# A planned attention kernel: final maxima queued at once, additions until the last pair, and another order of heads in the scores

## The chip, the cores and the metric

The kernel runs on one core of one Trainium2 chip. The metric is the time of one execution in microseconds on the device. Before the change it is 5001.09 us, the median of 3 runs (5000.94 to 5010.77). The core has five engines that run side by side, each with its own queue of instructions: TensorE (matrix products; "PE" in the profile, and "PEld" for its weight loads), VectorE (DVE), ScalarE (ACT), GpSimd (POOL) and SyncE (SP, which issues the transfers).

## The reference

The input x has 8 batches of 1024 rows of 512 numbers, and a context of 8 x 1024 x 384. Cut to what matters:

```
# layer 1: cross-attention to the context, 8 heads of 64
y = layernorm(x); q = y @ Wq; k = ctx @ Wk; v = ctx @ Wv
x = x + tanh(g1) * (softmax(q k^T / 8) v @ Wo + bo)

# layer 2: self-attention, 16 heads of 32, and a gate per row
y = layernorm(x); q, k, v = y @ Wq.T + bq, y @ Wk.T + bk, y @ Wv.T + bv
q = (q / |q| + query_embedding) * softplus(temperature)
h = softmax(q k^T / sqrt(32)) v
gates = softmax(h @ Wr.T + br), the 3 largest of 15 kept; sw = softmax(h @ Ws.T + bs)
weight = sum of 3 * gates * 2 sw[1], and 2 sw[0] * sum(sw)
x = x + tanh(g2) * ((h * weight) @ Wp.T + bp)
```

All of it is float32.

## The kernel before, in words

**Tiling.** A batch has 8 tiles of 128 rows. Features stand on the partitions in attention. A *chunk* (class `Chunk`, line 261) is 128 of the 512 head features: two heads of 64 in layer 1 (kind 1), four heads of 32 in layer 2 (kind 2). Each layer of each batch has four chunks, so there are 64 chunks, worked off one after the other. Queries are taken in two halves of 512.

**A chunk's steps.** `attention` (582) goes through the steps of a chunk: 8 in kind 1, 16 in kind 2. A step covers one half of the queries and two key tiles (kind 1) or one (kind 2). `score` (441) makes four score products of 128 keys x 512 queries, in two PSUM tiles of two each (`sc`, two buffers). The negative maximum of each query row is added by a product with one row of ones (`ones_b`, line 454), and then comes k times q. Each head has its own strip of 32 or 64 rows of the array. ScalarE takes the exponential of each of the two tiles (465). `value` (541) multiplies the exponentials with v (552), one step behind the scores: the scores of step m+1 are issued before the values of step m.

**The sums.** Softmax needs the sum of the exponentials over keys. GpSimd adds two exponential tiles (`paired`, 468 and 470: two key tiles in kind 1, the tiles of two steps in kind 2). Then `add` (474) either lets VectorE add the result to a running one (483), which frees a buffer, or keeps it as one more item. `summed` (493) reduces all kept items over the partitions with products with ones (503): a round of two or four products for every kept item. Its result's reciprocal comes from ScalarE (527, 528), and `divided` (531) multiplies the chunk's output with it, mostly on GpSimd. The exponential tiles have nine buffers; `room` (631) forces a reduction (`summed` with a partial result, 516 and 524) if too many are kept.

**The maxima.** While a chunk is attended to, the row maxima of the next one are found in bf16 (`maxima`, 371): pairs of score products (`pm`, 378; two heads each) and VectorE's maximum of each (419), or four at once in the wide form (402). In kind 2, pairs with n = 0 are of heads 0 and 1 and those with n = 1 of heads 2 and 3. At the end VectorE takes the negative maximum over all key halves (`nm`, 424), TensorE transposes it (`pr`, 428), ScalarE copies it (430), and four DMAs by SyncE (432) write it to rows of `sh`, which the scores of that chunk read.

**Order by a planner.** The order on TensorE, ScalarE, VectorE and GpSimd is the order in which the program issues the instructions. The program keeps a planned time for TensorE, VectorE and GpSimd in `at`, and each piece of work adds its planned cost. `attend` (674) interleaves the steps of a chunk with maxima pairs of the next chunk or the one after it (`pair`, 659) and with *fillers* (projections, output products, transposes of other stages). A pair is issued only if VectorE's planned time is not more than a given slack ahead of TensorE's; for the last two calls (`nm` and `pr`) the slack is 0. Work that others must finish first is put on lists with a due time (`later`, `soon`). `in_time` (701) tells by the number of pairs still to come whether VectorE may do additions in kind 2 and in batch 0; in kind 1 of later batches it may at all times. `pace` (978) does the same between the layers, and in the prologue, with fillers alone.

**The rest that is touched.** `gates` (828) makes the gate products (`pg`) of one half of the queries once the last chunk of that half is in `finished`. The prologue (1002 to 1026) normalises the eight tiles of batch 0, transposes them (`pt`, 218), and puts one tile of the context's v (`pv`) between two of these; then come the projections of the first chunks.

Of the kernel before, what the change touches and what calls it, by code (L numbers as in the profile page):

```python
# [10 lines left out]
F32 = mybir.dt.float32  # L11
# [5 lines left out]
P = 128  # L17
# [4 lines left out]
def tile_gated_block(  # L22
# [41 lines left out]
    NT = N // P  # L64
    ND = D // P
    NDC = DC // P
    H = 512
    NH = N // H
    NQ = NT // NH
# [155 lines left out]

    part = [False]

    columns = [HD2]
# [32 lines left out]
    class Chunk:  # L261
# [109 lines left out]
        def maxima(self):  # L371
# [35 lines left out]
            while todo:  # L407
                c, kh, n = todo.pop(0)
                if wide[0] and (kh if nh == 2 else n) == 0:
                    todo.pop(0)  # L410
                    four(c, kh)
                    self.done += 1
                    yield
                    continue
                at["PE"] = max(at["PE"], at["DVE"] - 700)
                for i in (2 * n, 2 * n + 1):
                    ps = gen(f"pm_{key}_{i}_{c}_{kh}")
                    scores(ps, c, i, kh)
                    nc.vector.tensor_reduce(mx[:, i * NT + c, kh : kh + 1], ps, AX.X, ALU.max)  # L419
                pe(PAIR)  # L420
                dve(2 * 690)
                yield
            nm = small.tile([P, nh * NT], F32, tag="nm", name=f"nm_{key}")
            nc.vector.tensor_reduce(nm, mx, AX.X, ALU.max, negate=True)
            dve(200)
            yield
            pr = ps_gen.tile([nh * NT, P], F32, tag="gen", name=f"pr_{key}")
            nc.tensor.transpose(pr, nm, ident)
# [11 lines left out]

        def score(self, step):

            h, s = step
            kind, nh, width, key = self.kind, self.nh, self.width, self.key
            pss = [
                ps_sc.tile([P, 2, H], F32, tag="sc", name=f"sc_{key}_{h}_{s}_{u}") for u in range(2)
            ]
            parts = [(i, kk) for kk in range(self.nk) for i in range(nh)]
            for m in range(2):
                for j, (i, kk) in enumerate(parts):  # L450
                    r, kc = i * width, s * self.nk + kk
                    if m == 0:
                        r += kk * HD2
                        lhsT, rhs = ones_b[r : r + 1, :], self.sh[r : r + 1, ts(h, H)]
                    else:
                        rows = slice(r, r + width)
                        lhsT, rhs = self.k[rows, ts(kc, P)], self.q[rows, ts(h, H)]
                    nc.tensor.matmul(  # L458
                        pss[j // 2][:, j % 2, :], lhsT=lhsT, rhs=rhs, start=(m == 0), stop=(m == 1)
                    )  # L460
            pe(self.SC)
            e = []
            for u in range(2):
                e.append(epool.tile([P, 2, H], F32, tag="e", name=f"e_{key}_{h}_{s}_{u}"))
                nc.scalar.activation(e[u], pss[u], AF.Exp)  # L465
            self.e[step] = e

# [63 lines left out]
        def divided(self, h, r=None):  # L531

            if h not in self.halves:
                self.halves[h] = r
                return
            self.finished.add(h)
            hT, r = self.st.hT[h][:, self.c, :], self.halves[h] if r is None else r
            engine = nc.vector if self.ends else nc.gpsimd
            engine.tensor_tensor(hT, hT, r, ALU.mult)
# [61 lines left out]

        def begun(self):
            self.whole = {}
            self.e, self.acc, self.parts, self.halves, self.finished = {}, {}, {}, {}, set()
            self.score(self.steps[0])


# [51 lines left out]
    def pair(ch, slack):  # L659

        if ch is None or ch.mx is None or at["PE"] < ch.free:
            return False
        if ch.done + 2 >= ch.pairs:
            slack = 0
        elif part[0]:
            slack = min(slack, 700)
        if at["DVE"] - at["PE"] > slack:
            return False
        ch.done += 1
        if next(ch.mx, "end") == "end":  # L670
            ch.mx = None
        return True

    def attend(
# [146 lines left out]
    def finish(st, other=None):  # L821
# [180 lines left out]
    st = begin(0)  # L1002
# [102 lines left out]
```

## Time and profile before

| | |
|---|---|
| median of 3 runs | 5001.09 us |
| profiled execution, its own time | 5004.68 us |
| its span, first to last instruction | 5002.9 us |
| mean granted clock of TensorE | 0.996 |
| TensorE busy | 4803.4 us (96%) |
| VectorE, GpSimd, ScalarE busy | 2988.2, 2567.5, 2309.3 us |
| additions of exponentials on VectorE (line 483) | x431, 760.1 us |
| sums on TensorE (line 503) | x1364 records, 204.2 us |

A row of the groups gives line, engine, operation, output and inputs, shapes and count, then busy time and the mean of one in ns, then idle time of the engine before these and what ended it. A row of the waits gives who waited for whom: us in total, times, and the longest. A row of the timeline gives the start and the duration in us, and in brackets the idle time before it. A row of the table by stretch gives its ends and length, the busy time of TensorE, its weight loads, VectorE, ScalarE and GpSimd with counts, the granted clock, the DMA share and GB/s. A float32 product leaves two records, a bf16 one leaves one.

### The profile page before, as it was taken

The page shows a single profiled execution, that of the slowest core. Times are in us where ns is not written, and L with a number is a line of the kernel's source. Part 1 is how long each engine was busy: PE and PEld are TensorE (multiplying, and loading weights), DVE is VectorE, ACT ScalarE, POOL GpSimd, SP SyncE. Part 2 cuts the span into 40 slices and gives each one's busy share as a digit, 9 for nine tenths or more (in the row PEclk, how much of TensorE's full clock was granted, in tenths as well). Part 3 has the DMA queues.
Part 4 walks back from the last instruction along what each step waited for, and adds up shares of the span by engine and source line. Part 5 has one row for each costly group of instructions (what it writes and reads, how often), then busy time and mean ns, then how long its engine had stood idle before and what let it go on. Part 6 is the DMA issues. An engine that isn't in the chain of part 4 may idle for free.

```text
span 5002.9 us, 83870 instructions
## 1 busy us (share of the span) xinstructions
PE 4803.4 (96%) x35660; PEld 1427.7 (29%) x35660; DVE 2988.2 (60%) x4111; ACT 2309.3 (46%) x3036; POOL 2567.5 (51%) x1346
## 2 busy tenths in 40 slices
PE   9999999999999999999999999999999999999998
PEld 2222232222322223222233222332223322233222
DVE  4657755577555775557745577555765557654664
ACT  3435634356343563435634356243652436524354
POOL 1635646356463663636636366363663636636464
PEclk9999999999999999999999999999999999999999
DMA  2000010000101001010010100101001010010000
GB/s 79 26 29 19 24 50 27 33 17 23 49 26 36 14 23 49 26 36 13 23 55 20 36 13 23 64 11 36 17 21 64 9 36 22 9 51 9 18 1 18
DMA packets 126280, 145.18 MB, mean 29 GB/s; under 512 B 14544, under 2 KB 75984, under 8 KB 125904
## 3 DMA queue, kind: packets, MB, share of 16 engines
q1 hardware_dynamic: 125616, 139.81, 8.8%
q8 instruction: 279, 4.57, 0.4%
q14 instruction: 97, 0.79, 0.1%
q10 hardware_dynamic: 288, 0.00, 0.0%
HBM read 122.47 MB, written 16.78 MB: 28 GB/s over the span
## 4 chain that ended last, share of the span: by engine, by line
PE 78%; DVE 9%; ACT 7%; issue 4%; POOL 2%; DMA 1%; SPq 0%; ACTq 0%; DVEq 0%; POOLq 0%
PE sc L458 21%; PE av L552 16%; PE po L247 8%; PE pq L247 8%; PE pm L378 7%; PE pk L247 6%; PE pv L247 6%; ACT e L465 5%; DVE mx L402 4%; PE sum L503 3%; DVE mx L419 3%; POOL e L470 2%; PE pt L218 1%; DVE e L483 1%; PE pn L247 1%
## 5 line engine op out<-in xcount | busy, mean ns | idle before, releaser
L470 POOL TENSOR_TENSOR e<-e,e 128x1024 f32<-128x1024 f32 x764 | 1859.3, 2448 | 1230.9 <-PE av L552 767.5
L465 ACT ACTIVATE e<-sc 128x1024 f32<-128x1024 f32 x1536 | 1490.3, 1021 | 1359.6 <-PE sc L458 1290.8
L419 DVE TENSOR_REDUCE mx<-pm 128x1 f32<-128x512 f32 x2336 | 1496.3, 685 | 981.6 <-PE pm L378 969.2
L458 PE MATMUL sc<-q,k 32*128 32x512 f32 (+1 forms) x6144 | 1113.2, 606 | 0.0
L552 PE MATMUL av<-e,v 128*32 128x512 f32 (+1 forms) x6144 | 1080.9, 611 | 0.0
L483 DVE TENSOR_TENSOR e<-e,e 128x1024 f32<-128x1024 f32 x431 | 760.1, 1779 | 347.2 <-POOL e L470 345.4
L378 PE MATMUL pm<-kb,qb 32*128 32x512 bf16 (+1 forms) x3072 | 625.5, 383 | 60.4 <-DVE mx L402 25.9
L402 DVE TENSOR_REDUCE mx<-pm 128x2 f32<-128x1024 f32 x368 | 425.3, 1218 | 290.5 <-PE pm L378 290.5
L458 PE MATMUL sc<-sh,ones_b 1*128 1x512 bf16 x3072 | 406.6, 384 | 76.0 <-ACT e L465 63.7
L458 PEld LDWEIGHTS sc<-q,k 32*128 32x128 f32 (+1 forms) x6144 | 422.6, 186 | 192.4 <-issue 186.2
L378 PEld LDWEIGHTS <-qb 32*128 32x128 bf16 (+1 forms) x3072 | 147.5, 92 | 941.7 <-issue 932.5
L552 PEld LDWEIGHTS av<-e,v 128*32 128x32 f32 (+1 forms) x6144 | 194.0, 117 | 621.2 <-issue 590.4
L247 PE MATMUL pq<-y1T,wq 128*32 128x512 f32 (+1 forms) x1568 | 248.0, 599 | 4.4 <-ACT k L333 2.5
L247 PE MATMUL pk<-y2T,wk 128*32 128x512 f32 x2048 | 242.6, 595 | 7.5 <-ACT qq L320 7.5
L247 PE MATMUL pq<-y2T,wq 128*32 128x512 f32 x2048 | 245.0, 596 | 2.8 <-ACT rn L345 2.8
L247 PE MATMUL pv<-wv,y2T 128*32 128x512 f32 x2048 | 241.3, 597 | 0.0
L247 PE MATMUL po<-wo,h1T 128*32 128x512 f32 x2048 | 229.7, 595 | 1.0
L247 PE MATMUL po<-wp,h2T 128*64 128x512 f32 (+1 forms) x1152 | 230.6, 597 | 0.0
L458 PEld LDWEIGHTS <-ones_b 1*128 1x128 bf16 x3072 | 100.3, 91 | 445.7 <-issue 427.9
L247 PE MATMUL pk<-ctx,wk 128*32 128x512 f32 (+1 forms) x1176 | 190.7, 607 | 17.9 <-DMA ctx<-in_ctx 6.6
L503 PE MATMUL sum<-e,ones 128*32 128x512 f32 (+1 forms) x1364 | 204.2, 596 | 0.0
L347 POOL TENSOR_TENSOR qq<-qq,rn 128x512 f32<-128x512 f32 x64 | 88.3, 1379 | 220.0 <-ACT rn L346 220.0
(109 smaller groups left out, 2871.0 us busy)
## 6 DMA issues: line engine op xcount, KB each, us to landing
x<-in_x SPq DMA_DIRECT2D x64, 256.0 KB
out<-x SPq DMA_DIRECT2D x64, 256.0 KB
xs<-in_x SPq DMA_DIRECT2D x56, 256.0 KB
xn<-in_x SPq DMA_DIRECT2D x56, 256.0 KB
ctx<-in_ctx SPq DMA_DIRECT2D x7, 1536.0 KB
wq<-in_L_xattn_Wq SPq DMA_DIRECT2D x32, 256.0 KB
wo<-in_L_xattn_Wo SPq DMA_DIRECT2D x8, 1024.0 KB
wk<-in_L_ffn_Wk SPq DMA_DIRECT2D x32, 256.0 KB
```

The costliest lines, as they stand in the source:

```text
L218: nc.tensor.transpose(pt[:, c, :], xn[:, ts(c, P)], ident)
L247: nc.tensor.matmul(ps[ts(j, w), :], lhsT=lhsT[:, ts(j, w)], rhs=rhs, start=start, stop=stop)
L347: nc.gpsimd.tensor_tensor(self.qq, self.qq, rn, ALU.mult)
L378: nc.tensor.matmul(ps, lhsT=self.qb[ts(i, width), ts(c, P)], rhs=self.kb[ts(i, width), ts(kh, H)], start=True, stop=True,)
L402: nc.vector.tensor_reduce(out, tiles[u], AX.X, ALU.max)
L419: nc.vector.tensor_reduce(mx[:, i * NT + c, kh : kh + 1], ps, AX.X, ALU.max)
L458: nc.tensor.matmul(pss[j // 2][:, j % 2, :], lhsT=lhsT, rhs=rhs, start=(m == 0), stop=(m == 1))
L465: nc.scalar.activation(e[u], pss[u], AF.Exp)
L470: nc.gpsimd.tensor_tensor(one, one, two, ALU.add)
L483: nc.vector.tensor_tensor(accs[-1], accs[-1], a, ALU.add)
L503: nc.tensor.matmul(ps[ts(2 * u + j, self.width), :], lhsT=ones[:, 0 : self.width], rhs=acc[n][:, j, :], start=(n == 0), stop=(n == len(acc ...
L552: nc.tensor.matmul(self.av[ts(i, width), :], lhsT=st.v[:, kc, ts(self.c * self.nh + i, width)], rhs=e[j // 2][:, j % 2, :], start=(kc == 0 ...
```

## The change

There are six edits.

1. `pair`: the two last calls of a chunk's maxima are no longer held back by VectorE's planned time. `nm` is issued at the next chance, and sets `free` to VectorE's planned end plus 300 ns; the transpose `pr` is issued once TensorE's planned time has reached that.
2. `in_time`: additions are allowed when fewer than two calls are left (only `pr`, or nothing); the bound on pairs is three per step rather than two while a chunk of kind 1 is attended to; the reserve is 7000 ns rather than 10000.
3. `score`: if the last maxima pair issued before it had n = 0 and the chunk is of kind 2, the two PSUM tiles, their products and their exponentials are taken in the order heads 2, 3 and then 0, 1. `value` and the additions keep their order.
4. `divided` notes the planned time at which a half was finished, and `gates` waits until 2500 ns of planned TensorE time after it (not once the last chunk is through).
5. Prologue: the first query projection half stands ahead of the sixth tile's place among the transposes, and there is no v tile in the eighth; the two v tiles left over come later.
6. `pace` in the prologue counts six more products as left.

```diff
@@ maxima @@
+                taken[0] = n == 0
                 pe(PAIR)
                 dve(2 * 690)
                 yield
             nm = small.tile([P, nh * NT], F32, tag="nm", name=f"nm_{key}")
             nc.vector.tensor_reduce(nm, mx, AX.X, ALU.max, negate=True)
             dve(200)
+            self.free = at["DVE"] + 300
             yield
@@ score @@
-            pss = [
-                ps_sc.tile([P, 2, H], F32, tag="sc", name=f"sc_{key}_{h}_{s}_{u}") for u in range(2)
-            ]
-            parts = [(i, kk) for kk in range(self.nk) for i in range(nh)]
+            order = (1, 0) if taken[0] and self.kind == 2 else (0, 1)
+            taken[0] = False
+            pss = {
+                u: ps_sc.tile([P, 2, H], F32, tag="sc", name=f"sc_{key}_{h}_{s}_{u}") for u in order
+            }
             for m in range(2):
-                for j, (i, kk) in enumerate(parts):
+                for j in (2 * u + v for u in order for v in range(2)):
+                    kk, i = divmod(j, nh)
                     r, kc = i * width, s * self.nk + kk
...
-            for u in range(2):
-                e.append(epool.tile([P, 2, H], F32, tag="e", name=f"e_{key}_{h}_{s}_{u}"))
+            e = {}
+            for u in order:
+                e[u] = epool.tile([P, 2, H], F32, tag="e", name=f"e_{key}_{h}_{s}_{u}")
                 nc.scalar.activation(e[u], pss[u], AF.Exp)
@@ divided @@
-            self.finished.add(h)
+            self.finished[h] = at["PE"]
@@ pair @@
-        if ch.done + 2 >= ch.pairs:
-            slack = 0
-        elif part[0]:
-            slack = min(slack, 700)
-        if at["DVE"] - at["PE"] > slack:
-            return False
+        if ch.done + 2 < ch.pairs:
+            if at["DVE"] - at["PE"] > (min(slack, 700) if part[0] else slack):
+                return False
@@ in_time @@
-            steps = (1 - share) * len(ch.steps)
-            return pairs <= 2 * steps - 3 and work <= (1 - share) * (1.1 * total + cost) - 10000
+            steps = (1 - share) * len(ch.steps) * (2 if ch.kind == 2 else 3)
+            return pairs < 2 or pairs <= steps - 3 and work <= (1 - share) * (1.1 * total + cost) - 7000
@@ gates @@
-            while h not in st.chunks[2][-1].finished:
+            done = st.chunks[2][-1].finished
+            while h not in done or not st.through and at["PE"] < done[h] + 2500:
                 yield
@@ prologue @@
-        run(values, NDC * MM)
+        if t == NQ + 1:
+            run(fill, ND * MM)
+        elif t < NT - 1:
+            run(values, NDC * MM)
...
-    pace(one[0], fill, one[1], (14 + 14) * MM)
+    pace(one[0], fill, one[1], (6 + 14 + 14) * MM)
```

More of the change, by code (lines that the diff above doesn't have):

```diff
@@ L226, in tile_gated_block @@
     part = [False]
+    taken = [False]
     columns = [HD2]
@@ L443, in score @@
             h, s = step
-            kind, nh, width, key = self.kind, self.nh, self.width, self.key
-            pss = [
-                ps_sc.tile([P, 2, H], F32, tag="sc", name=f"sc_{key}_{h}_{s}_{u}") for u in range(2)
-            ]
-            parts = [(i, kk) for kk in range(self.nk) for i in range(nh)]
+            nh, width, key = self.nh, self.width, self.key
+            order = (1, 0) if taken[0] and self.kind == 2 else (0, 1)
[3 more added lines that the diff above has]
+            }
             for m in range(2):
-                for j, (i, kk) in enumerate(parts):
+                for j in (2 * u + v for u in order for v in range(2)):
+                    kk, i = divmod(j, nh)
                     r, kc = i * width, s * self.nk + kk
@@ L461, in score @@
             pe(self.SC)
-            e = []
-            for u in range(2):
-                e.append(epool.tile([P, 2, H], F32, tag="e", name=f"e_{key}_{h}_{s}_{u}"))
+            e = {}
+            for u in order:
+                e[u] = epool.tile([P, 2, H], F32, tag="e", name=f"e_{key}_{h}_{s}_{u}")
                 nc.scalar.activation(e[u], pss[u], AF.Exp)
@@ L603, in begun @@
             self.whole = {}
-            self.e, self.acc, self.parts, self.halves, self.finished = {}, {}, {}, {}, set()
+            self.e, self.acc, self.parts, self.halves, self.finished = {}, {}, {}, {}, {}
             self.score(self.steps[0])
```

## The prediction

> **What bounds the kernel now.** I read the page first (busy time and clock by slice), then TensorE's waits, then the timeline at places that the change touches. The page:
>
> ```profile
> span 5002.9 us, 83870 instructions
> PE 4803.4 (96%) x35660; PEld 1427.7 (29%) x35660; DVE 2988.2 (60%) x4111; ACT 2309.3 (46%) x3036; POOL 2567.5 (51%) x1346
> ...
> PE 78%; DVE 9%; ACT 7%; issue 4%; POOL 2%; DMA 1%; SPq 0%; ACTq 0%; DVEq 0%; POOLq 0%
> ...
> L503 PE MATMUL sum<-e,ones 128*32 128x512 f32 (+1 forms) x1364 | 204.2, 596 | 0.0
> ```
>
> TensorE is busy 96% and holds most of the chain; all its idle time is 5002.9 - 4803.4 = 200 us. Time falls only by less work on TensorE or fewer of its waits. VectorE has 40% to spare. The last row is the work that the change takes away: sums of exponentials over keys, as products with ones. The waits of TensorE that the change touches:
>
> ```profile
> PE sc L458 <- ACT e L465: 63.7, 155, 2.1
> PE pm L378 <- DVE mx L419: 21.6, 36, 2.6
> PE sc L458 <- DMA sh<-rows: 10.6, 20, 2.5
> PE pg L247 <- DVE h2T L539: 2.9, 1, 2.9
> ```
>
> None is large: at most 10.6 and 2.9 us can be won at the last two.
>
> **Part 1: additions allowed to the last pair (in_time).** In the built order the sums on TensorE fall from 682 to 590 products, and VectorE's additions rise from 431 to 477. By the tiles: in each batch 0 to 6 the sum of the last second-layer chunk's second half was two groups of 8 products (four rounds of four, in four column strips) and becomes one group of 4 (one round): 3 rounds x 7 = 21. The first chunk of all goes from four rounds to one: 3. In all 24. What a round costs:
>
> ```profile
> 2507.49 1.07 PE L552 MATMUL av<-e,v 128*32 128x512 f32 x8
> 2508.37 1.90 PE L503 MATMUL sum<-e,ones 128*32 128x512 f32 x16
> 2510.09 1.04 PE L247 MATMUL pq<-y1T,wq 128*32 128x512 f32 x8
> ```
>
> From 2508.37 to 2510.09 two rounds took 1.72, so 0.86 each (x16, as each f32 product leaves two records). 24 x 0.86 = 20.6; seven groups fewer, which alone take 0.97 rather than 0.86, 0.8 more: -21.4. Seven partial sums also lose their copy (ScalarE) and their 0.69-us addition (VectorE), off the path.
>
> What of this is given back? Behind this sum come three steps with only scores and values (2.2 us of TensorE), in which scores wait 0.52 us for exponentials. The step that loses the sum has 3.0 us left against 3.17 of the score-exponential-score round trip (2514.42 to 2517.58 between second-half scores), so it gives back about 0.15, and the next chunk's first step, from which a maxima pair moves away, about 0.2: 7 x 0.35 = +2.5. The new order of maxima pairs and projections among steps is worth a little less switching, about -0.5 in all. Part 1: -19.4.
>
> VectorE pays 46 x 1.78 us (row L483: 760.1/431) = 82 us. Does that hold up TensorE? Six additions per batch stand behind the last maximum of the next chunk, ahead of the maxima after it:
>
> ```profile
> 2505.43 0.19 DVE L424 TENSOR_REDUCE nm<-mx 128x16 f32<-128x32 f32 x1
> 2521.24 1.29 DVE L419 TENSOR_REDUCE mx<-pm 128x1 f32<-128x512 f32 x2 [15.63 <-PE pm L378]
> ```
>
> VectorE stood idle for 15.63 us just there. Six additions at this stretch's mean of 2.41 us (slowed beside GpSimd) take 14.4. The last two need GpSimd's pair at 2516.83 to 2521.49, which moves 1.8 earlier with the values before it: done by about 2522. The sum now stands after six projection products of the next chunk's second step, by my count at 2525.7. Cover 3 us; if it were gone, maxima and then TensorE would be late by what is missing. I take 0.
>
> **Part 2: the final maximum at once, its transpose when due.** Its DMAs (four, by SyncE, unchanged in number) start earlier where the old rule waited for VectorE's planned idleness. Prologue: the transpose stood last before the first scores; now 4 maxima and 24 projection products (5.8 us) follow it, and it took 4.1 us from the transpose at 80.45 to the last landing. So its two waits (2.49 + 0.98) go: -3.5. At the last chunk it moves ahead of one value step (1.0): -1.0. Elsewhere it moves by half a step, with nothing waiting.
>
> Such waits also cost clock:
>
> ```profile
> 80.00:92.00 12.00, 8.31 (x33) 2.36 (x27) 1.29 (x2) 2.78 (x4) 1.04 (x1) 0.72 0.08 24
> ...
> 4940.00:4958.00 18.00, 14.99 (x230) 5.57 (x233) 6.21 (x25) 7.84 (x12) 5.74 (x3) 0.81 0.01 2
> ```
>
> The granted clock is the third number from the end. 12 x (1 - 0.72) = 3.4 us lost after the first scores' wait, 18 x 0.19 = 3.4 after the 2.90 us of the gates. The Trainium skill (TensorE: Matmul & The Clock Gate, the table of what matters for your kernels) speaks against counting them: only idle gaps over some 3 us, about one window of 3.4, would throttle; by it the gates' 2.90 would cost nothing. The row decides: such waits lose about as much again. By the rule Parts 2 and 3 would be 7 us smaller.
>
> **Part 3: gates later.** At the end gates leave 2.5 us of planned work behind the last division; one score and value step (2.0) moves ahead of the wait of 2.90. -2.0 of the wait, and the clock's 3.4 at even odds, -1.7. In other batches no gate waited.
>
> **Part 4: prologue order.** Six of eight value tiles now lie among the transposes, with the first query half after the fourth. TensorE had no gap there. The query product needs the copy of the fourth transpose just before it (0.7 late); the last two transposes come without a product between, so the eighth waits for its normalisation (1.6 by ScalarE's order: Ln, Exp, 0.81 scale after the copy before); the second query half waits for the last copy (0.7). +3.0, between +1 and +6.5 (with a 3.4 clock loss). Late next is nothing: the DMA wait that followed is gone.
>
> **Part 5: first batch.** With three rounds fewer and GpSimd's division placed after another addition, the wait of 2.59 us for VectorE at 129 (an addition there waited for GpSimd behind that division) may go, with a 3.4 clock loss. Between 0 and -6; I take -3.
>
> **Part 6: score order.** 296 of the 512 second-layer steps begin with heads 2, 3, of which 266 stand just behind a pair of heads 0, 1. The Trainium skill (TensorE: Matmul & The Clock Gate, Part 3, what overlaps) says matmuls are strictly first in, first out. Then heads 0, 1 would block heads 2, 3 behind the maxima for 0.21 us, and the new order would win 266 x 0.21 = 56. The trace, first behind maxima of heads 2, 3, then of 0, 1 (heads from the built order):
>
> ```profile
> 1026.15 0.39 PE L378 MATMUL pm<-kb,qb 32*128 32x512 bf16 x2
> 1026.15 0.60 PE L458 MATMUL sc<-sh,ones_b 1*128 1x512 bf16 x4
> ...
> 1027.54 1.07 PE L552 MATMUL av<-e,v 128*32 128x512 f32 x8
> ...
> 1034.46 0.39 PE L378 MATMUL pm<-kb,qb 32*128 32x512 bf16 x2
> 1034.48 0.59 PE L458 MATMUL sc<-sh,ones_b 1*128 1x512 bf16 x4
> ...
> 1035.86 1.06 PE L552 MATMUL av<-e,v 128*32 128x512 f32 x8
> ```
>
> 1.39 and 1.40 us to the next values: the same. In the second, too, two of the four products start 0.02 us after the maxima, so other strips pass. Worth 0, not -56. Where scores wait for an exponential, the following maxima of heads 2, 3 could start 0.1 earlier; where that isn't inside the exponentials' round trip (some 40 steps), up to -4. Against it: GpSimd's first addition of a step pair takes heads 0, 1, whose exponential is now second, 0.92 us later (1.02 minus overlap). Its waits for exponentials (407.0 us, 163 times) average 2.5, which covers that. Between -4 and +6; I take -1.
>
> **Sum.** -19.4 - 4.5 - 3.4 (prologue clock) - 3.7 + 3.0 - 3 - 1 = -32. Stalls that an order of 27,000 instructions hides I set at +4: **-28**. The profiled execution ran 5004.7 with a span of 5002.9, 3.6 above the median of 5001.1; against the median: **4973**.
>
> **Rivals.** (a) Only the sums count: the prologue's new stalls eat its gain, the clock is lost elsewhere, no end gain: -19.4 and up to +8 of new waits, 4982 to 4990. For it: the waits of Part 2 are few and some of the time comes back as ScalarE's round trip. Against: the DMA wait clearly has cover now. (b) Slower: GpSimd becomes the bound in second-layer steps. Each swapped pair starts 0.92 later; once its idle before a pair is under 0.92, exponentials lack buffers (ScalarE already waits 10.1 us for these). Half the 512 steps are pairs, some 148 touched; exposed in a third, +45 against -28: 5018. It decides from 30 pairs on (28/0.92). Against: 4.7 of 6.3 us per pair busy. (c) No difference: the order is swapped at a cost that meets the sums, 5001.
>
> **How the numbers follow.** Forecast (4960 to 4981) 0.58, rival (a) 0.28, (c) 0.06, (b) 0.08. Faster takes the first two: 0.86; same 0.06; slower 0.08. Under 0.2% (10 us) a measurement can't tell from no change. Range: all ends of Parts 2 to 6 favourable give 4959; (a) with its waits gives 4990: 4959 to 4990, leaving out (b), (c).
>
> **What would show it.** Sums x1180 on TensorE, busy about 28 us less in that row; additions x477; no wait of scores for the rows' DMA near 80 us; no half clock there; six additions in VectorE's 15-us gap and sums not waiting for them; equal step times behind either pair of heads. Wrong if GpSimd's or ScalarE's waits for buffers grow by tens of us, or if TensorE waits for VectorE's maxima in each batch.

## The result, and the profile after

The changed kernel takes 4964.44 us (median of 6 runs, 4963.06 to 4964.79), the kernel before 5005.48 us beside it (5000.94 to 5010.77): a ratio of 0.9917, with a 95% interval from 0.9904 to 0.993. It is faster by 0.83%. The forecast was 4973 in a range of 4959 to 4990.

The page of the changed kernel (busy time by engine, the chain that ended last, one group of instructions):

```profile
span 4962.6 us, 83502 instructions
PE 4751.6 (96%) x35476; PEld 1413.5 (28%) x35476; DVE 3126.6 (63%) x4148; ACT 2307.6 (47%) x3029; POOL 2571.3 (52%) x1346
...
PE 78%; DVE 10%; ACT 6%; issue 3%; POOL 2%; DMA 0%; SPq 0%; ACTq 0%; DVEq 0%; POOLq 0%
...
L491 DVE TENSOR_TENSOR e<-e,e 128x1024 f32<-128x1024 f32 x477 | 897.7, 1900 | 319.0 <-POOL e L478 317.4
```

TensorE is still the bound. The span fell by 5002.9 - 4962.6 = 40.3 us and TensorE's busy time by 4803.4 - 4751.6 = 51.8, so its idle time even grew by 11. A product that runs at half clock counts at its stretched length, so the 51.8 is not all removed work. The trace records 45.0 us at half clock in the profiled execution before and 20.8 in the changed one; half of that is lost, 22.5 and 10.4. So about 12 of the 40 us are clock. The sums' own row, from the groups:

```profile
L511 PE MATMUL sum<-e,ones 128*32 128x512 f32 (+1 forms) x1180 | 183.1, 596 | 0.1
```

That is 204.2 - 183.1 = 21.1 us less for 184 fewer records, the count that was forecast. The waits of TensorE, for the whole span:

```profile
PE sc L466 <- ACT e L473: 87.2, 161, 3.7
...
PE sc L466 <- DMA sh<-rows: 11.1, 22, 2.5
...
PE pm L380 <- DVE mx L421: 8.5, 37, 0.4
...
PE pg L249 <- DVE h2T L547: 0.7, 1, 0.7
```

The wait for maxima fell from 21.6 to 8.5 and its longest from 2.6 to 0.4; the gates' wait fell from 2.9 to 0.7; the rows' transfer is waited for as long as before, 11.1 against 10.6; and the wait for exponentials rose from 63.7 to 87.2. The last was not forecast. The stretch near 80 us, in the table by stretch, has no half clock any more (third number from the end, 0.72 before):

```profile
80.00:92.00 12.00, 11.43 (x78) 3.35 (x66) 4.37 (x7) 5.07 (x6) 2.02 (x2) 1.00 0.08 24
```

**Where the 40 us came from.** The order on TensorE is fixed, so the start of each step's scores can be compared step by step between kernels; undisturbed steps agree within 0.02 us. Of the 40.3 us of span, 14.4 lie in the prologue and the first batch, 7.1 in the last batch, and 18.8 in the six between. Some large differences only move work: in the first chunk of each later batch the third step is shorter by 6.08 us, and the fifth and seventh are longer by 1.33 and 3.00. The largest that repeats and is not of this kind is in a step for which nothing was forecast: the seventh step of the last second-layer chunk, in six of the batches 0 to 6 (in batch 2 the gain shows two steps later). In batch 3 it took 5.50 us before and takes 3.36 now. The timeline before, at that step (VectorE, GpSimd and the maxima's products):

```profile
2473.61 6.66 DVE L483 TENSOR_TENSOR e<-e,e 128x1024 f32<-128x1024 f32 x2
2476.70 5.79 POOL L470 TENSOR_TENSOR e<-e,e 128x1024 f32<-128x1024 f32 x2 [0.81 <-ACT e L465]
...
2480.19 2.47 DVE L419 TENSOR_REDUCE mx<-pm 128x1 f32<-128x512 f32 x4
2480.92 0.37 PE L378 MATMUL pm<-kb,qb 64*128 64x512 bf16 x1 [1.77 <-DVE mx L419]
```

VectorE's two additions take 6.66 us, so the maxima behind them come late, and a maxima product of TensorE waits 1.77 us for a free buffer. After the change, at the same step (in narrow stretches, so that each addition shows alone):

```profile
2452.65 3.37 DVE L491 TENSOR_TENSOR e<-e,e 128x1024 f32<-128x1024 f32 x1
...
2455.95 1.21 DVE L491 TENSOR_TENSOR e<-e,e 128x1024 f32<-128x1024 f32 x1
2456.59 2.79 POOL L478 TENSOR_TENSOR e<-e,e 128x1024 f32<-128x1024 f32 x1 [1.65 <-ACT e L473]
```

The second addition takes 1.21 us because GpSimd's pair starts 0.64 us behind it. In the kernel before, GpSimd's pair was first. The question for the experiments was which of the six edits did this, and what each of the others is worth.

### The profile page after: what moved, and what is told of

It reads as the page before. It is cut to its first block, busy times and chain, and to the rows that moved or that the text cites. A ratio compares the mean times of both kernels' runs of the same rounds, so it can differ in the third digit from the quotient of the medians.

```text
span 4962.6 us, 83502 instructions
## 1 busy us (share of the span) xinstructions
PE 4751.6 (96%) x35476; PEld 1413.5 (28%) x35476; DVE 3126.6 (63%) x4148; ACT 2307.6 (47%) x3029; POOL 2571.3 (52%) x1346
## 4 chain that ended last, share of the span: by engine, by line
PE 78%; DVE 10%; ACT 6%; issue 3%; POOL 2%; DMA 0%; SPq 0%; ACTq 0%; DVEq 0%; POOLq 0%
PE sc L466 20%; PE av L560 16%; PE po L249 8%; PE pq L249 8%; PE pk L249 7%; PE pm L380 7%; PE pv L249 6%; DVE mx L404 4%; ACT e L473 4%; PE sum L511 3%; DVE mx L421 3%; DVE e L491 2%; POOL e L478 2%; PE pt L218 1%; PE pn L249 1%
## 5 line engine op out<-in xcount | busy, mean ns | idle before, releaser
L491 DVE TENSOR_TENSOR e<-e,e 128x1024 f32<-128x1024 f32 x477 | 897.7, 1900 | 319.0 <-POOL e L478 317.4
L466 PE MATMUL sc<-sh,ones_b 1*128 1x512 bf16 x3072 | 408.2, 383 | 99.9 <-ACT e L473 87.2
L249 PE MATMUL pv<-wv,ctx 128*32 128x512 f32 x1536 | 194.2, 596 | 5.4 <-ACT v L793 5.4
```

Source lines behind the costliest of these rows:

```text
L249: nc.tensor.matmul(ps[ts(j, w), :], lhsT=lhsT[:, ts(j, w)], rhs=rhs, start=start, stop=stop)
L466: nc.tensor.matmul(pss[j // 2][:, j % 2, :], lhsT=lhsT, rhs=rhs, start=(m == 0), stop=(m == 1))
L491: nc.vector.tensor_tensor(accs[-1], accs[-1], a, ALU.add)
```

## The experiments

Each kernel is timed beside the kernel before on the same chip. "Undone" means the changed kernel without that edit, "alone" the kernel before with that edit only.

| kernel | median us | against the changed (4964.4) or the one before (5005.5) |
|---|---|---|
| score order undone | 4985.2 | +20.8 |
| new rule for additions undone | 4970.1 | +5.7 |
| final maximum at once, undone | 5053.5 | +89.1 |
| prologue undone | 4974.4 | +9.9 |
| later gates undone | 4968.0 | +3.5 |
| score order alone | 4977.1 | -28.4 |
| new rule for additions alone | 5085.2 | +79.7 |
| final maximum at once, alone | 4999.3 | -6.2 |

The edits don't add up: the value of two of them differs by some 80 us according to whether the other is there. The medians of the kernel before that were taken beside these runs lie between 5004.2 and 5007.3, so medians alone don't tell differences of some 3 us between two rows apart; where that matters, step times are compared.

### The score order undone

```diff
-            order = (1, 0) if taken[0] and self.kind == 2 else (0, 1)
+            order = (0, 1)
```

> The changed kernel with the score products always in the order heads 0, 1 and then 2, 3; everything else, 590 sum products included, stays. Theory (TensorE lets products on other strips pass, so the order is worth about nothing): 4966 us, between 4960 and 4971, and the steps behind a pair of heads 0, 1 take the same time as before within 0.05 us. Rival A (strictly first in, first out): 0.21 us at each of 266 steps comes back, 5020 us. Rival B (the order is what took away the wait of 1.8 us for VectorE's maxima in the seventh step of the last second-layer chunk of each batch): that wait is back in seven batches, 4977 us.

It took 4985.23 us (4984.27 to 4986.02; ratio to before 0.996, 0.9945 to 0.9975). The strict order in and out falls: it would have given 5020, and the steps behind a pair of heads 0, 1 take the same 3.36 us in both kernels. "Worth nothing" falls as well. The wait for maxima is back, as the waits show:

```profile
PE sc L466 <- ACT e L473: 67.8, 157, 2.1
...
PE pm L380 <- DVE mx L421: 19.5, 37, 2.1
```

Its timeline at the step, in narrow stretches:

```profile
2465.34 2.48 POOL L478 TENSOR_TENSOR e<-e,e 128x1024 f32<-128x1024 f32 x1 [0.82 <-ACT e L473]
...
2465.52 3.38 DVE L491 TENSOR_TENSOR e<-e,e 128x1024 f32<-128x1024 f32 x1
2467.78 3.34 POOL L478 TENSOR_TENSOR e<-e,e 128x1024 f32<-128x1024 f32 x1
```

VectorE's addition starts 0.18 us behind GpSimd's. GpSimd's first takes nearly its usual time (2.48; two undisturbed take 4.67), VectorE's takes 3.38 and not 1.21 and ends 1.08 after GpSimd's first; and GpSimd's second, begun meanwhile, takes 3.34. The Trainium skill (SBUF — State Buffer, Who interferes with whom) says that the two engines share one pair of ports under an exclusive lock. The rows fit that: whichever begins first runs, and the other stands still. So a start that is moved by a fraction of a microsecond decides whether VectorE needs 1.2 or 3.4 us.

But the wait for exponentials fell too, from 87.2 to 67.8: part of what the order wins at the maxima it loses there.

### Whether it is GpSimd's start or TensorE's order

The new order does two things: it swaps the products and exponentials, and it holds GpSimd's pair back, since that still begins with heads 0, 1. Two kernels take these apart. In the first GpSimd follows the exponentials:

```diff
-                for u in range(2):
-                    self.paired(h, s + 1, u, e[u], self.e[h, s + 1][u], u == 1)
+                for n, u in enumerate(self.e[h, s + 1]):
+                    self.paired(h, s + 1, u, e[u], self.e[h, s + 1][u], n == 1)
```

> The changed kernel, TensorE's and ScalarE's order of work untouched, but GpSimd's two additions of a step pair follow the order of the exponentials (heads 2, 3 first where these come first), so that its pair is no longer held back by about 0.8 us. Theory (the swap of the scores gains only because it holds GpSimd's pair back, so that VectorE's second addition in the seventh step of the last second-layer chunk runs alone in 1.21 us and not beside GpSimd in 3.37): the wait of 1.8 us for the maxima returns in seven batches with its half clock, as in the run without the score order, 4983 us. Rival (the order of the products on TensorE is what gains): 4964 us, no such wait.

In the second the scores keep the order 0, 1 and GpSimd always takes heads 2, 3 first (`enumerate((1, 0))` in the same place, and `order = (0, 1)`):

> The changed kernel with the scores always in the order heads 0, 1 and then 2, 3 (as in the run that gave 4985), and GpSimd's additions of a step pair always in the other order, so that each pair of it waits for the second exponential. Theory (holding GpSimd back is the gain): no wait of 1.8 us for maxima in the last second-layer chunks, 4966 us, within 6. Rival A (the order on TensorE is the gain): 4985 us. Rival B (held back in every pair, GpSimd becomes the bound, 0.9 us in part of 256 pairs): above 5000 us.

The first took 4971.90 us (4970.73 to 4973.30), the second 4971.99 (4966.80 to 4972.30; the profiled one is the 4966.80). At the step in question the two differ clearly. GpSimd following, TensorE's order as changed:

```profile
2455.97 6.66 DVE L491 TENSOR_TENSOR e<-e,e 128x1024 f32<-128x1024 f32 x2
2459.10 5.75 POOL L478 TENSOR_TENSOR e<-e,e 128x1024 f32<-128x1024 f32 x2 [0.85 <-ACT e L473]
...
2463.28 0.37 PE L380 MATMUL pm<-kb,qb 64*128 64x512 bf16 x1 [1.76 <-DVE mx L421]
```

GpSimd held back, TensorE's order as before:

```profile
2453.55 4.50 DVE L491 TENSOR_TENSOR e<-e,e 128x1024 f32<-128x1024 f32 x2
...
2457.47 5.12 POOL L478 TENSOR_TENSOR e<-e,e 128x1024 f32<-128x1024 f32 x2 [1.64 <-ACT e L473]
```

The step takes 5.50 us in the first and 3.36 in the second. So GpSimd's later start takes the wait away, and the products' order has no part in it. In the totals both count: 4985 us with neither, 4972 with either one, 4964 with both. My totals were wrong all the same: I expected 4983 for the first kernel and it took 4972. Three things bear on it.

First, the products' order does gain something elsewhere. Between the first of these two kernels and the one without the score order only the order of products, exponentials and GpSimd's pairs differs. Over the first three second-layer chunks of a batch the steps differ by -0.40 + 0.25 - 0.90, near -1 us, 7 in seven batches. It comes in pieces of 0.1 to 0.3 us, at steps that wait for an exponential and at others that wait for nothing; why is not shown. (The first step of the third chunk looks like more, 3.86 us in the old order and 3.03 in the new, but the step before it is 0.76 longer: the first scores now stand behind the wait for the rows' transfer.)

Second, the 1.8-us wait is there in both kernels, but in the profiled executions a half clock follows it at 5 of the 7 places without the score order and at 2 where GpSimd follows, which is another 5 us.

Third, what GpSimd's delay wins it mostly gives back. Against the changed kernel, the one in which GpSimd follows loses 1.6 us in each last second-layer chunk (and up to 1.7 more where a half clock follows), but wins 1.26 or about 2.2 in the next first-layer chunk. Of the 7.5 us between the two, most (4.4 in the profiled executions) lie in the last batch, which was not taken apart. The changed kernel, at the start of that first-layer chunk in batch 4:

```profile
2489.35 11.91 DVE L491 TENSOR_TENSOR e<-e,e 128x1024 f32<-128x1024 f32 x4 [3.30 <-POOL e L478]
...
2492.58 5.63 POOL L478 TENSOR_TENSOR e<-e,e 128x1024 f32<-128x1024 f32 x2 [0.96 <-PE av L560]
2492.80 1.02 ACT L473 ACTIVATE e<-sc 128x1024 f32<-128x1024 f32 x1 [0.43 <-DVE e L491]
...
2493.87 0.39 PE L466 MATMUL sc<-sh,ones_b 1*128 1x512 bf16 x2 [1.06 <-ACT e L473]
```

Four of VectorE's six additions in a row take 11.91 us here, about 3 each. ScalarE waits for one of them to free an exponential tile, and TensorE waits 1.06 us for ScalarE. Where GpSimd follows, the same step has half that wait, 0.52 us, as in the kernel before. The wait of 1.06 stands at all seven such places of the changed kernel: in three of them a half clock follows (about 2.2 us lost in all), in the other four a second wait of 0.52 in the next step (1.26 lost).

### Holding GpSimd back where it pays

If the delay gains in the first half of that chunk and costs in the second, the second half can do without:

```diff
-                for u in range(2):
-                    self.paired(h, s + 1, u, e[u], self.e[h, s + 1][u], u == 1)
+                us = self.e[h, s + 1] if st.b + 1 < B and self.c == 3 and h == 1 else (0, 1)
+                for n, u in enumerate(us):
+                    self.paired(h, s + 1, u, e[u], self.e[h, s + 1][u], n == 1)
```

> The changed kernel, where GpSimd's pair follows the order of the exponentials in one place only, the second half of the last second-layer chunk of batches 0 to 6; in the first half and all else it stays heads 0, 1 first. Theory (holding GpSimd back gains in the first half, by the 1.8-us wait for maxima that it avoids, and costs in the second, by about 1.06 us of waits for exponentials at the start of the next first-layer chunk): these waits go, 7 x 1.06, with a half clock or two: 4957 us. Rival (those waits come from the order of the exponentials themselves, or from the six additions): 4964 us.

It took 4955.11 us (4954.12 to 4956.04; ratio to before 0.9899, 0.9884 to 0.9913), 9.3 less than the changed kernel. The same place:

```profile
2483.13 4.50 DVE L491 TENSOR_TENSOR e<-e,e 128x1024 f32<-128x1024 f32 x2 [2.63 <-POOL e L478]
...
2487.20 4.95 POOL L478 TENSOR_TENSOR e<-e,e 128x1024 f32<-128x1024 f32 x2 [1.78 <-PE av L560]
2487.95 0.39 PE L466 MATMUL sc<-sh,ones_b 1*128 1x512 bf16 x2 [0.53 <-ACT e L473]
...
2489.86 5.34 DVE L491 TENSOR_TENSOR e<-e,e 128x1024 f32<-128x1024 f32 x2 [2.24 <-POOL e L478]
```

The four additions come in two pairs of 4.50 and 5.34 us. The second of the four starts ahead of GpSimd's and takes 1.21 us, where it took 3.38 in the changed kernel; TensorE's wait is 0.53. The chunk is shorter by 1.0 to 2.2 us in every batch from 1 to 7. ScalarE's waits for tiles that VectorE's additions free are 10.1 us in the kernel before, 20.0 in the changed one and 8.0 here. So it was GpSimd's timing that the six additions ran into, not their number.

### The final maximum at once, undone

```diff
-        if ch.done + 2 < ch.pairs:
-            if at["DVE"] - at["PE"] > (min(slack, 700) if part[0] else slack):
-                return False
+        if ch.done + 2 >= ch.pairs:
+            slack = 0
+        elif part[0]:
+            slack = min(slack, 700)
+        if at["DVE"] - at["PE"] > slack:
+            return False
```

(and without the line that sets `self.free` behind `nm`)

> The changed kernel with the old rule for the last two maxima calls (held back while VectorE's planned time is ahead). The prologue stays as changed, to the last product. The sums go from 590 to 618 products, 7 rounds. Theory (this edit is worth its rounds and little else, since the prologue's cover is not its doing): +6 + 0.5, 4971 us, and no wait of the first scores for the rows' transfer near 80 us. Rival A (the prediction's Part 2: the prologue's wait of 3.5 us and half clock of 3.4 us come back with it): 4978 us. Rival B (this edit took away the 1.8-us wait for maxima in the last second-layer chunk of each batch): 4983 us.

It took 5053.51 us (5049.64 to 5056.16), 89 more than the changed kernel and 48 more than the one before. None of the three expectations comes near. There is indeed no wait near 80 us, and the step of the 1.8-us wait stays at 3.36. The waits show what is new:

```profile
PE sc L465 <- ACT e L472: 76.8, 146, 3.7
PE sc L465 <- DMA sh<-rows: 51.8, 40, 3.6
```

The rows' transfer costs 51.8 us rather than 11.1. The timeline at the end of the second second-layer chunk of batch 3:

```profile
2396.35 0.22 DVE L427 TENSOR_REDUCE nm<-mx 128x32 f32<-128x64 f32 x1
...
2399.14 0.28 PE L431 MATMUL pr<-ident,nm 128*32 128x128 f32 x1
...
2401.23 2.70 SPq L435 DMA_DIRECT2D sh<-rows  x4
2404.35 0.39 PE L465 MATMUL sc<-sh,ones_b 1*128 1x512 bf16 x1 [3.61 <-DMA sh<-rows]
```

and in the changed kernel:

```profile
2351.97 0.22 DVE L427 TENSOR_REDUCE nm<-mx 128x32 f32<-128x64 f32 x1
...
2354.44 0.28 PE L432 MATMUL pr<-ident,nm 128*32 128x128 f32 x1
...
2359.83 0.39 PE L466 MATMUL sc<-sh,ones_b 1*128 1x512 bf16 x1 [0.56 <-DMA sh<-rows]
```

From `nm` to the scores it is about 8 us in both kernels, of which 5.2 to 5.4 are from the transpose on (with copy and transfer). In the changed kernel TensorE has work for all of it but 0.56 us, under the old rule for all but 3.61. In TensorE's order the old rule puts the last pair of maxima and the transpose later, the transpose into the chunk's last step instead of the last but one. Half clocks follow many of the waits of 2 to 3.6 us: the mean granted clock is 0.987 against 0.998, which is 5054 x 0.011 = 56 us and so more than half of the loss. That VectorE's planned additions hold the last calls back is what the rule says; that they do so here, the order shows, not a measured wait.

### The two rules, each alone

The new rule for additions on the kernel before:

```diff
-            steps = (1 - share) * len(ch.steps)
-            return pairs <= 2 * steps - 3 and work <= (1 - share) * (1.1 * total + cost) - 10000
+            steps = (1 - share) * len(ch.steps) * (2 if ch.kind == 2 else 3)
+            return pairs < 2 or pairs <= steps - 3 and work <= (1 - share) * (1.1 * total + cost) - 7000
```

> The kernel before with the new rule for VectorE's additions alone. The sums go from 682 to 624 products, 14.5 rounds. Theory (the rule needs the final maximum queued at once: without that, additions let in before the final maximum hold it and its rows back, as in the run with the old pair rule): the rows' transfer is waited for at the starts of second-layer chunks and at the second first-layer chunks, some 40 waits of 50 us in all with half clocks behind them, 5060 us. Rival A (the prediction: the rule is worth its rounds): -12.5 us, 4990 us. Rival B (what cost in that run came with the score order): below 5000 us.

The new rule for the last two calls on the kernel before (the reverse of the diff above):

> The kernel before with the final maximum queued at once, alone. The sums go from 682 to 640 products, 10.5 rounds. The first products up to the first scores are those of before. Theory (worth its rounds; the prologue keeps its wait): -9 us, 4995 us. Rival A (the prediction's Part 2 besides, prologue's wait and clock): -16 us, 4988 us. Rival B (without the new rule for additions the maxima come at a worse place): 5005 us or more.

The additions alone took 5085.15 us (5083.76 to 5090.82; ratio 1.016, 1.0145 to 1.0175): slower, although 58 products of sums are gone. The waits:

```profile
PE sc L458 <- DMA sh<-rows: 46.2, 56, 2.6
```

It is the theory's wait, with 56 places and 46 us (mean clock 0.986), and 25 us more than the 5060 I had set. The last two calls alone took 4999.25 us (4996.91 to 5002.07; ratio 0.9985, 0.9978 to 0.9992): 6.4 less than the kernel before beside it, a little under the rounds' -9; the prologue keeps its wait. So the rule for additions pays only with the final maximum queued at once; the two are one edit in effect.

### The new rule for additions, undone

The reverse of the diff above, in the changed kernel.

> The changed kernel with the old rule for when VectorE may add (bound of two pairs per step, reserve 10000, nothing special for the last two calls). The sums go from 590 to 634 products, 11 rounds. Theory (a round is 0.86 us, but the six additions in a row behind the last maximum cost about 1.5 us per batch in exponentials without a buffer, which comes back): +9.5 - 10, 4964 us, no measurable difference. Rival A (the prediction's size, 0.35 us given back per batch): +9.5 - 1, 4973 us. Rival B (this rule is also what took away the 1.8-us wait for maxima in the last second-layer chunk): 4973 + 12 = 4985 us.

4970.09 us (4968.32 to 4970.93), +5.7, between the theory and rival A. The sums rise to 634 products, 11 rounds, 9.5 us. The waits for exponentials didn't fall (90.5 us, and the wait of 1.06 stands at all seven places), so the theory's reason for a smaller loss, the six additions, is refuted. Instead the second-layer chunks of the last batch are shorter by 4.7 us in all; without these the loss would be 10.4, about the rounds' price. What makes them shorter shows in the last experiment below.

### The prologue undone

```diff
-        if t == NQ + 1:
-            run(fill, ND * MM)
-        elif t < NT - 1:
-            run(values, NDC * MM)
+        run(values, NDC * MM)
...
-    pace(one[0], fill, one[1], (6 + 14 + 14) * MM)
+    pace(one[0], fill, one[1], (14 + 14) * MM)
```

> The changed kernel with the old prologue (a tile of v between each two transposes, and the old count of products left in the wide maxima). Its first products are those of the kernel before, up to the first scores. The sums go from 590 to 596 products (three rounds in the first chunk). Theory (the prologue's edits alone gave the cover for the rows' transfer): wait +3.5, half clock +3.4 near 84 us, three rounds +2.6, the new stalls among the transposes gone -3.0: 4971 us. Rival (the new final-maximum rule gives the cover, and the prologue's new order only costs): 4961 us.

4974.35 us (4971.10 to 4981.84), +9.9, near the theory. The new rule for the final maximum is in this kernel, and the wait is there:

```profile
78.91 0.19 DVE L427 TENSOR_REDUCE nm<-mx 128x16 f32<-128x32 f32 x1
80.18 0.28 PE L432 MATMUL pr<-ident,nm 128*16 128x128 f32 x1
...
82.92 0.39 PE L466 MATMUL sc<-sh,ones_b 1*128 1x512 bf16 x1 [2.46 <-DMA sh<-rows]
```

The transpose stands last before the scores although `nm` is queued at once: in TensorE's order all the prologue's projections are ahead of it. The table by stretch for this kernel shows the clock:

```profile
80.00:92.00 12.00, 8.30 (x27) 2.37 (x25) 1.29 (x2) 2.78 (x4) 1.04 (x1) 0.65 0.08 24
```

12 x 0.35 = 4.2 us are lost here. This run takes back both edits of the prologue (5 and 6), so it doesn't say which of them gives the cover. The wait of 2.6 us for maxima in the first chunk is in this kernel too. In the changed kernel the prologue has these waits instead (waits of the first 84 us):

```profile
PE pt L218 <- ACT xn L203: 1.7, 1, 1.7
PE pq L249 <- ACT y1T L219: 1.4, 2, 0.7
```

### The gates undone

```diff
-            while h not in done or not st.through and at["PE"] < done[h] + 2500:
+            while h not in done:
```

> The changed kernel with the old condition for the gates (as soon as the half is divided). In TensorE's order only the last chunk of the last batch differs: the gates stand one score and value step earlier and wait. Theory (the prediction's Part 3): the wait of 2.9 us for the divided output is back, +2.0, and at times its half clock, +1.7: 4967 us. Rival (the wait only moves, since what follows the gates waits for the same exponentials): 4964.5 us.

4967.98 us (4966.31 to 4971.89), +3.5. The wait is back at its old size:

```profile
PE pg L249 <- DVE h2T L547: 2.9, 1, 2.9
```

2.9 - 0.7 = 2.2 us is wait; that the rest is clock is an inference by subtraction. The ranges don't overlap with the changed kernel's, but 3.5 us is 0.07%, hardly more than the medians of the kernel before differ.

### The score order alone

The diff of `score` in the change, and `taken`, on the kernel before.

> The kernel before with the new order of the scores alone; its 682 sum products stay. Theory (GpSimd held back takes away the 1.8-us wait for maxima in the last second-layer chunks here as well, -2.1 per batch, some 1.1 comes back at the start of the next chunk, and the products' order gains about 0.9 per batch at steps that wait for exponentials): 7 x -1.9, and -5 in the last batch as in the other runs: 4987 us. Rival A (the swap only helps beside the other edits): 5005 us. Rival B (the prediction's -1): 5004 us, between 5001 and 5011. Rival C (strictly first in, first out): 4950 us.

4977.09 us (4974.93 to 4978.30; ratio 0.9943, 0.9926 to 0.9959): 30 less than the kernel before beside it (5007.28). The step of the 1.8-us wait falls from 5.50 to 3.36 here as well, and nothing is given back in the next chunk (its first step stays at 4.47), where VectorE has no six additions in a row. That fits its being worth more alone than beside the others, where undoing it cost 21:

```profile
PE sc L463 <- ACT e L470: 77.5, 155, 3.7
...
PE pm L380 <- DVE mx L421: 10.8, 37, 2.6
```

The wait for maxima halves, as in the changed kernel.

### The old rule for additions in the last batch

On top of the kernel that took 4955:

```diff
+            if ch.st.b + 1 == B:
+                steps = (1 - share) * len(ch.steps)
+                return pairs <= 2 * steps - 3 and work <= (1 - share) * (1.1 * total + cost) - 10000
```

> The kernel that held GpSimd back in the first half only (4955 us), with the old rule for VectorE's additions in the last batch alone; 596 sum products. In the run with the old rule everywhere, the last batch's second-layer chunks took 4.7 us less than in the changed kernel, half clocks included. Theory (in the last batch no next chunk's fillers cover the waits that the new rule moves): 4951 us. Rival (that gain was the chance of a few half clocks): 4955 us, within 1.5.

4950.50 us (4948.79 to 4951.03; ratio 0.989, 0.9873 to 0.9906). It is the fastest kernel of this study, 14 us below the changed one. Of the 4.6 us between it and the 4955 the medians alone prove little, since the kernel before beside it was also 3 us faster. The steps are clearer: batches 0 to 6 agree within 0.2 us, and the last is shorter by 3.4. Its last three second-layer chunks are shorter by 4.4 together, most of it (2.6) in the last step of the third. There the transpose stands. Without the old rule (the 4955):

```profile
4852.03 0.28 PE L432 MATMUL pr<-ident,nm 128*32 128x128 f32 x1
...
4855.84 0.39 PE L466 MATMUL sc<-sh,ones_b 1*128 1x512 bf16 x1 [2.53 <-DMA sh<-rows]
```

and with it:

```profile
4850.14 0.28 PE L432 MATMUL pr<-ident,nm 128*32 128x128 f32 x1
...
4854.30 0.39 PE L466 MATMUL sc<-sh,ones_b 1*128 1x512 bf16 x1 [0.33 <-DMA sh<-rows]
```

With the old rule the transpose comes ahead of the step's scores and not behind them, so TensorE has those scores to do while the rows are on their way. The wait of 2.53 us for the rows is gone (0.63 is left over the four products), and so is the half clock right behind it; one further on in the batch is longer. The wait of 2.53 stands in the kernel before and in the changed one too; in the run of the last two calls alone and in that with the new rule for additions undone, 0.63 is left of it as here.

## Why the prediction was right, and where it was not

The time fell inside the range, 8.6 us below the number; against the kernel before beside it the change is worth 41 us where 28 were forecast. The parts of its sum were less right than the sum, and that the total stayed inside the range is partly luck: Part 6 gained some 20 us more than it was given, Part 1 some 4 less, and the new rule for additions, which costs 80 us by itself, came together with the edit that it needs.

**Part 1 (sums), -19.4.** The 24 rounds are gone (the three of the first chunk are of two products each, and two products more go in the last batch: 84 + 6 + 2 = 92), and a step that loses two of them is shorter by 1.93 us (from 4.97 to 3.04), 0.97 a round. The row's busy time fell by 21.1 us, close to the 21.4 of the sum; the 28 named among the signs does not follow from it. But the give-back of 0.35 us per batch was sized too small. Between the kernel before and the one with all but the score order, a batch's steps without half clocks add up to about -1.7 us where three rounds at 0.97 promise -2.9, so about 1.2 are given back. The largest piece sits where I didn't look: two steps of the first second-layer chunk, in which pairs of maxima and the transpose changed places, take 0.15 and 0.66 us more. -1.7 x 7, with the three rounds of the first chunk (2.6, worked out, not isolated), gives about -15. And the step named only the rule for additions: alone that rule costs 80 us.

**Part 1's cover.** The six additions did run in VectorE's gap and were done in time (in batch 4 the last at 2501.3, the sum at 2505.6). The missing item was another one: an addition also frees the exponential tiles that ScalarE writes, and TensorE waits for these. The changed kernel pays 1.0 to 2.2 us for it at each of seven places, by the run that takes it away.

**Part 2 (final maximum at once), -3.5 - 1.0 - 3.4.** The wait near 80 us, its size and its clock were right, and given to the wrong edit: the run with the old prologue keeps the wait, the one with the old rule for the last two calls doesn't. The 1.0 at the last chunk did not come: its longest wait for the rows is 2.53 us in both kernels, because the new rule for additions takes back there what this edit gives. "Elsewhere it moves by half a step, with nothing waiting" is the step that failed worst. It was read from the trace before, and holds there (-6 alone, with 10.5 rounds gone); beside the new additions the same edit is worth 89.

**Half clocks.** I weighed the rule of the Trainium skill (TensorE: Matmul & The Clock Gate, the table of what matters for your kernels: no idle gaps over some 3 us) against the row near 80 us and took the row. The runs confirm the row: with the old prologue, waits of 2.46 and 1.02 us have 0.65 of the clock behind them. Shorter waits go against the rule too. Of nine profiled kernels with the new prologue, eight have a half clock for 3.4 us near 40 us, behind waits of 1.7, 0.7 and 0.7. Behind the 1.8-us waits for maxima, 2 of 7 places show one in the kernel before and 5 of 7 in the run without the score order; behind the 1.06-us waits for exponentials it is 3 of 7 in the changed kernel. Each is 3.4 us at half, 1.7 us lost. What decides at which places it happens is not shown.

**Part 3 (gates), -3.7.** Undoing it cost 3.5, with the uncertainty named above.

**Part 4 (prologue order), +3.0.** The waits are 1.7 and 1.4, together 3.1; the half clock near 40 us adds 1.7, inside the given range.

**Part 5 (first batch), -3.** The wait of 2.6 us is gone, and so is the half clock behind it (0.76 of the clock from 126 to 140 us before, 14 x 0.24 = 3.4): 6 us, the far end of the given range. But the wait stays in the kernel with the old prologue, so it was given to the wrong edit.

**Part 6 (score order), -1.** This is the term that was mis-sized: it is worth 21 to 28 us (some 13 by GpSimd's delay alone, as much by the order alone). Rejecting the strict first in, first out was right. What failed is the sentence "Against it: GpSimd's first addition of a step pair takes heads 0, 1, whose exponential is now second, 0.92 us later". The delay was counted as a cost alone; it moves GpSimd behind VectorE, and VectorE's addition from 3.4 to 1.2 us. What the products' order gains by itself was bounded at -4 and is nearer -7; whether that comes by earlier maxima, as Part 6 had it, was not taken apart.

Rival (b), GpSimd's delay starving ScalarE of buffers, was a real mechanism with a price of some 9 us (4964.4 against 4955.1), not 45: ScalarE's waits for the tiles of VectorE's additions are 20.0 us in the changed kernel and 10.2 without the score order. The path was another one: GpSimd's delay slowed VectorE's additions, and these held the buffers. The +4 for unforeseen stalls was far from what two edits can do to one another, but they came together.

## What to carry to other kernels

When VectorE and GpSimd both do additions of two inputs from SBUF, look at which starts first: here the later one stood still. Delaying the engine that has slack can be worth as much as removing work: 13 us where the delay stands alone, against some 15 for the sums. A part of a change that looks idle in the old trace may be what makes another part harmless; undo it in the new kernel, not only try it in the old one. Look up what an instruction frees, not only what it computes: here a late addition delayed an exponential, not a sum.

## What was not expected of the hardware

An addition of 128 x 1024 on VectorE takes 1.21 us alone and 3.37 beside GpSimd's, whose own goes from 2.34 to 3.34 when it is the one that stands still. A delay of 0.83 us in GpSimd's start, relative to the step, decides which.

The clock isn't only taken after waits of three microseconds: stretches of 3.4 us at half clock follow waits of 1.06 to 1.8 us at some places and not at others. That goes with the scatter of the times: the kernel with GpSimd reversed took 4966.8 us in one execution, with a mean granted clock of 0.999, and about 4972 in three, with 0.997.
